# Perceiver block on one Trainium2 core: where the first contexts are loaded and turned, and in which order the queries are folded

## Chip, core and metric

The kernel runs on one core of a Trainium2 chip. The metric is the device time of one execution in microseconds (us). Three runs of the kernel before gave 2559.17, 2561.69 and 2563.82 us; the median is 2561.69 us.

## What is computed

A block of three residual steps on x (32 sequences of 64 tokens, 256 channels), with a context of 1601 tokens of 192 channels for each sequence, all in float32:

```python
x = x + xattn(layernorm(x), ctx_768)   # 16 heads of 64; q from x, k and v from the context
x = x + attn(layernorm(x))             # RWKV-like scan over time, three 256x256 projections in, one out
x = x + ffn(layernorm(x))              # 256 -> 1024 -> 256 with relu
```

Here only the first step matters. For each sequence and head it is softmax(q k^T / 8) v, with q = layernorm(x) w_q, and k, v from ctx_768 w_kv.

## The kernel before

**Folding.** The kernel never forms the keys. It multiplies each head's query by that head's key weights once, which gives a folded query of 192 channels (128 "lo" and 64 "hi" ones), and scores it against the raw context. This is `queries`, called once for each group of 8 sequences (`tg` 0 to 3), in two halves of 8 heads (`e` 0 and 1). Each half, called (tg,e) below, is on TensorE: 4 query projections into PSUM tag "ps" (L292, 2 buffers, copied by ScalarE to `room[1]`, L299), the lo folding (L313, PSUM tag "f" with 6 buffers, two for each head pair, copied by VectorE, L320, and ScalarE, L321, into one of two `q_lo` buffers), scores of the single last context token (`odd_scores`, L250, from group 1 on once in each half, and twice in (0,1)), and the hi folding (L341, copied at L348 to L352). The folded queries go to DRAM (`q_dram`) by SyncE: two stores of 1 MB for lo (L323), numbered lo0 to lo15 over the whole folding, and two of 0.5 MB for hi (L355). In the second half the next group's normalised x is turned (`turned_x`, L208, L211); `normed_x` of the group after that (L119, L110, L197) is queued on VectorE behind that copy.

**Attention.** 64 units `u` (32 sequences b, two halves of the heads j). `scores` runs 6 steps of matmuls (L658) of the turned context `cT` with the folded query `q`; ScalarE copies each step to `s_sb` (L665, two buffers, tag "s_sb"), VectorE keeps a running maximum (L667, L669). At the first step of a sequence `rest_scores` (L635) does the keys that don't fill a block. Then the maximum over partitions on GpSimd (L684), subtraction (L703) and exp (L704); one unit later `av_lo` (L468) and `av_hi` (L864) multiply by the context `c`, framed by `left` (L809, L819). `total` (L766 to L770) and `inverse` (L784 to L788) make the denominators, and `keep` (L794) sends them to DRAM from ScalarE's queue.

**Loads.** `blocks_load` (L170, 12 transfers, 1.2 MB in pieces of 128 bytes) brings the context as 32x32 blocks `cb`; `ctx_prep` turns them on VectorE (L372 three times, L373 once) into `cT` and ends with a small transfer from partitions 64-127 to 0-63 (L374). `ctx_load` (L143) brings `c`, 1.15 MB; `rows_load` (L152) four small transfers; `q_load` (L180) 1.5 MB of folded queries.

**What sets the order.** All these transfers are issued by SyncE, in one queue, in order. Each engine also executes a fixed list in order. A compiler's scheduler makes that list: it takes what it thinks is ready, and the kernel constrains it by `tc.issue_after(ins)`, which puts what the block traces on the same engine behind `ins` in that engine's list, without a wait for its end. The folding's queries may run ahead of the folding itself: nothing holds L292 of the next half back but its PSUM buffers and `room[1]`.

**Memory.** `room` is the two `s_sb` buffers before the attention needs them. The odd scores `od` use one of the two `cT` buffers; so only `cT` of sequence 0 is turned within the folding, and that of sequence 1 in unit 1. The four stores of each half of the last group's odd scores (L264) are put off (`odd_late`) until unit 0's other loads have been issued.

Of the kernel before, what the change touches and what calls it, by code (L numbers as in the profile page):

```python
# [9 lines left out]
F32 = mybir.dt.float32  # L10
# [5 lines left out]
P = 128  # L16
# [4 lines left out]
def kernel(  # L21
# [38 lines left out]
    nc = tc.nc  # L60

    B, T, D = x.shape
# [63 lines left out]
    with ExitStack() as st_b:  # L126
        with ExitStack() as st_a:
# [20 lines left out]
            def rows_load(b):  # L148

                for r0 in (0, C2):  # L150
                    for n, cs in ((0, slice(0, P)), (1, slice(P, C))):
                        nc.sync.dma_start(  # L152
                            rows[b % 2][r0 : r0 + KR, n, n * C2 : P], ctx_768[b, KC * P : NK - 1, cs]
                        )

            def blocks_load(b):

                c = cpool.tile([P, NS, NBL, BL], F32, tag="cb", name=f"cb_{b}")
                for k in range(2):
# [78 lines left out]
            def odd_scores(tg, e, kodT, qTs, od, sps):  # L242

                po = [
                    sps.tile([P, TG], F32, tag="f", name=f"odd_ps_{tg}_{e}_{o}", bufs=6)
                    for o in range(2)
                ]
                for k in range(4):
                    for o in range(2):
                        nc.tensor.matmul(  # L250
                            po[o][k * B : (k + 1) * B, :],
                            lhsT=kodT[o * HD : (o + 1) * HD, 4 * e + k, :],
                            rhs=qTs[k // 2][o * HD : (o + 1) * HD, k % 2, :],
                            start=True,
                            stop=True,
                        )
                nc.vector.tensor_copy(od[:, 0, :], po[0])
                nc.scalar.copy(od[:, 1, :], po[1])
# [9 lines left out]
            def queries(tg, xnT, copied, sp, sps, wq_sb, wkT, room, codn, kodT, wk_lo, wk_hi, od):  # L268
# [7 lines left out]
                for e in range(NP // 4):  # L276
# [5 lines left out]
                    for g in (2 * e, 2 * e + 1):  # L282
                        slot = (tg * NP // 2 + g) % 5
                        qT = room[1][:, slot * 2 * TG : (slot + 1) * 2 * TG].rearrange(
                            "p (k t) -> p k t", k=2
                        )
                        qTs.append(qT)
                        for k in range(2):
                            hp = 2 * g + k
                            pq = sps.tile([P, TG], F32, tag="ps", name=f"q_ps_{tg}_{hp}")  # L290
                            for c in range(2):
                                projected = nc.tensor.matmul(  # L292
                                    pq,
                                    lhsT=wq_sb[:, c, hp * P : (hp + 1) * P],
                                    rhs=xnT[:, c, :],
                                    start=(c == 0),
                                    stop=(c == 1),
                                )
                            nc.scalar.activation(qT[:, k, :], pq, AF.Copy, scale=HD**-0.5)  # L299
                    if e == 0 and tg == 0:  # L300
                        with tc.issue_after(projected.ins):
# [24 lines left out]
                        )  # L326
                    all_q.append(qTs)
                    for n in (0, 1) if e == 1 and tg == 0 else (e,) if tg else ():
                        odd_scores(tg, n, kodT, all_q[n], od[n], sps)
                        if more:  # L330
                            odd_store(tg, n, od[n])
                        else:
                            odd_late.append(lambda n=n: odd_store(tg, n, od[n]))
                    for k in range(2):
                        ph = [
                            sps.tile([P, QB, T], F32, tag="f", name=f"qh_ps_{tg}_{e}_{k}_{o}", bufs=6)
                            for o in range(2)
                        ]
                        for n in range(2):
                            for o in range(2):  # L340
                                nc.tensor.matmul(  # L341
                                    ph[o][n * C2 : (n + 1) * C2, :, :],
                                    lhsT=wkT[o * HD : (o + 1) * HD, 4 * e + 2 * n + k, P:C],
                                    rhs=qTs[n][o * HD : (o + 1) * HD, k, :],
                                    start=True,
                                    stop=True,
                                )
                        nc.vector.tensor_copy(hi[:, :, 2 * k, :], ph[0])  # L348
                        if e == 1 and not more:
                            nc.scalar.copy(hi[:, :, 2 * k + 1, :], ph[1])  # L350
                        else:
                            nc.vector.tensor_copy(hi[:, :, 2 * k + 1, :], ph[1])  # L352
                    for n in range(2):
                        ns = slice((8 * e + 4 * n) * T, (8 * e + 4 * n + 4) * T)
                        store = nc.sync.dma_start(  # L355
                            q_dram[tg][:, P:C, ns].rearrange("b p n -> p b n"),
                            hi[n * C2 : (n + 1) * C2].rearrange("p b h t -> p b (h t)"),
                        )
                    if e == 0 and tg == 0:
                        pk = sps.tile([P, NP, BL], F32, tag="f", name="kod_ps", bufs=6)  # L360
                        turned_keys(kodT, wk_lo, wk_hi, pk)
                return following, store

            def ctx_prep(b):
# [12 lines left out]
            with tc.tile_pool(name="setup", bufs=1) as sp, tc.tile_pool(  # L377
# [11 lines left out]
                ]  # L389
                wk_hi, codn = wk_hi[0:C2], codn[0:B]  # L390
                kodT = kodT.rearrange("p (h b) -> p h b", b=B)
                od = kp.tile([P, NS * KT], F32, tag="cT", name="od")
                od = [
                    od[:, k * 2 * TG : (k + 1) * 2 * TG].rearrange("p (o t) -> p o t", o=2)
                    for k in range(2)
                ]
                wq_sb = wq_sb.rearrange("p (c n) -> p c n", c=2)
                wkT = wkT.rearrange("p (h c) -> p h c", c=C)
                wqr = w_q.rearrange("(c p) n -> p c n", p=P)
# [10 lines left out]
                for n in range(4, NT, 4):  # L410
                    nc.sync.dma_start(x_sb[:, n : n + 4, :], xr[:, n : n + 4, :])
                b_tiles = {0: blocks_load(0)}
                odd_late = []
                for g in range(NP // 2):
                    ps = sps.tile([P, 2, C], F32, tag="ps", name=f"wkT_ps_{g}")
                    for k in range(2):
# [8 lines left out]
                for tg in range(B // QB):  # L425
                    turned, store = queries(tg, *turned, sp, sps, wq_sb, wkT, room, codn, kodT, wk_lo, wk_hi, od)
                    if tg == 1:
                        q_tiles = {0: q_load(0)}
                        cT = ctx_prep(0)

            nats = {}
            aw = st_a.enter_context(tc.tile_pool(name="late", bufs=1))
# [528 lines left out]
                        x_sb[:, i, :], x_sb[:, i, :], bias_rows[:, 0, :], ALU.add  # L961
                    )

            c_tiles = {}
            rests = [None, None]
            last = None
            before = None
# [2 lines left out]
            for u in range(2 * B):  # L970
# [2 lines left out]
                phase, i = (u - 5) % 4, (u - 5) // 4  # L973
                if before is not None:
                    before.out()
                if j == 0:
                    rows_load(b)
                out, mixer, older = outs[max(i, 0)], mixers[max(i, 0)], mixers[max(i - 1, 0)]
                fill = {}
# [18 lines left out]
                if u == 1:  # L998

                    hooks = {3: parts[0:2], 4: parts[2:3], 5: parts[3:]}  # L1000
                elif last is not None:
                    hooks = {
                        3: [last.inverse] + ([out.share] if phase == 1 and i >= 0 else []),
                        5: [last.keep],
                    }
                    last.total()
                else:
                    hooks = {}
                s_sb, mx, top, done = scores(u, cT, q_tiles[b], hooks)
                if j == 0 and b + 1 < B:  # L1010
                    with tc.issue_after(store.ins):
                        b_tiles[b + 1] = blocks_load(b + 1)
                        q_tiles[b + 1] = q_load(b + 1)
                mb = max_all(u, mx)
                if u == 1:
                    with tc.issue_after(top.ins):
                        cT_next = ctx_prep(1)
                if last is not None:
                    last.av_lo(fill, done)
                parts = exps(u, s_sb, rests[j], mb)  # L1020
# [4 lines left out]
                if u == 1:  # L1025
                    last.total()
                    last.inverse()
                    last.keep()
                if j == 0 and 0 < b < B - 1:
                    cT_next = ctx_prep(b + 1)  # L1030
                elif j == 1:
                    cT = cT_next
                if phase == 0 and i > 0:
# [4 lines left out]
                    out.vproj()  # L1038
                if phase == 1 and i >= 0:
                    mixer.norm()  # L1040
                if j == 0:
                    c_tiles[b] = ctx_load(b)
                if phase == 3 and i >= -1:
                    odd_load(i + 1)
# [150 lines left out]
```

## Time and profile before

| | us |
|---|---|
| median of three runs | 2561.69 |
| the profiled execution: its time | 2561.88 |
| its span (first to last instruction) | 2560.1 |
| TensorE busy in the span | 2536.7 (99%) |
| VectorE busy | 1925.9 (75%) |
| ScalarE busy | 985.5 (38%) |
| GpSimd busy | 410.7 (16%) |
| folding: first query projection to first score matmul | 13.07 to 136.10 |
| first score matmul of unit 2 | 192.59 |
| first score matmul of unit 4 | 266.59 |

"PE" is TensorE's matmul row, "PEld" its weight loads, "DVE" VectorE, "ACT" ScalarE, "POOL" GpSimd, "SP" SyncE (a "q" behind an engine is its instruction queue). In a timeline row the columns are start in us, duration in us, engine, line, operation, output<-input, shapes, count; in brackets stand the engine's idle time before it and what ended it. A float32 matmul leaves several records, so a count is of records. In a row of stretches the columns are the stretch, its length, each engine's busy time with its number of instructions, then the clock granted to TensorE (1.00 is full), the busy share of the DMA engines (it can exceed 1 where packets overlap), and GB/s.

### The profile page before, as it was taken

What the parts mean: (1) busy time and instruction counts of PE and PEld (TensorE: products, weight loads), DVE (VectorE), ACT (ScalarE), POOL (GpSimd) and SP (SyncE); (2) the same over time, 40 slices, a digit from 0 to 9 for tenths busy, and PEclk for the clock granted to TensorE, in tenths of its full rate; (3) what the DMA queues carried; (4) which work ended last, traced back from release to release, by engine and by line L of the source; (5) the groups of instructions that cost most, each with busy time, mean ns of one, the idle gap of its engine ahead of it and who ended that gap; (6) DMA issues with size and microseconds to landing.
All of it is one profiled execution on the core that took longest, in us unless ns stands there. A gap on an engine that the chain in (4) does not pass through costs nothing.

```text
span 2560.1 us, 38115 instructions
## 1 busy us (share of the span) xinstructions
PE 2536.7 (99%) x15618; PEld 1216.5 (48%) x15618; DVE 1925.9 (75%) x2364; ACT 985.5 (38%) x1103; POOL 410.7 (16%) x372
## 2 busy tenths in 40 slices
PE   9989999999999999999999999999999999999999
PEld 3344444444444454444444444444444444444466
DVE  5477778878787878878787878778787878787731
ACT  3343434434333444343443334344343334343221
POOL 1002111111111111111111111111111111211100
PEclk9999999999999999999999999999999999999999
DMA  8796333233332323233332323323332322210100
GB/s 209 218 207 110 61 62 65 48 66 65 62 63 59 58 42 66 47 66 66 65 66 53 69 43 55 67 48 65 66 65 55 67 59 52 54 47 2 52 13 21
DMA packets 435967, 174.23 MB, mean 68 GB/s; under 512 B 334960, under 2 KB 421520, under 8 KB 435792
## 3 DMA queue, kind: packets, MB, share of 16 engines
q1 hardware_dynamic: 435408, 171.53, 33.1%
q8 instruction: 122, 2.00, 0.3%
q14 instruction: 53, 0.43, 0.1%
q10 hardware_dynamic: 384, 0.26, 0.0%
HBM read 141.07 MB, written 29.10 MB: 66 GB/s over the span
## 4 chain that ended last, share of the span: by engine, by line
PE 91%; DVE 3%; issue 2%; DMA 1%; SPq 1%; POOL 1%; ACT 1%; DVEq 0%; ACTq 0%; POOLq 0%
PE s_ps L658 36%; PE o_lo L468 24%; PE o_hi L864 12%; PE y_ps L468 3%; PE q_ps L292 2%; PE h_ps L1106 2%; PE fy L1120 2%; PE rest_ps L635 2%; PE o_hi L819 1%; PE v_ps L917 1%; PE ql_ps L313 1%; PE o_lo L809 1%; DVE s_sb L703 1%; PE v_ps L931 1%; DVE m L669 1%
## 5 line engine op out<-in xcount | busy, mean ns | idle before, releaser
L658 PE MATMUL s_ps<-q,cT 64*128 64x512 f32 x4608 | 1009.3, 591 | 1.2 <-ACT q_hi L350 0.8
L658 PEld LDWEIGHTS s_ps<-q,cT 64*128 64x128 f32 x4608 | 444.1, 187 | 516.1 <-issue 498.3
L468 PE MATMUL o_lo<-s_sb,c 128*64 128x512 f32 x3024 | 678.5, 596 | 5.6 <-DMA c<-in_ctx_dram 5.6
L665 ACT COPY s_sb<-s_ps 128x1024 f32<-128x1024 f32 x384 | 388.3, 1011 | 743.9 <-PE s_ps L658 735.8
L703 DVE TENSOR_TENSOR s_sb<-s_sb,mb 128x2048 f32<-128x2048 f32 x192 | 431.7, 2285 | 0.0
L704 ACT ACTIVATE s_sb<-s_sb 128x2048 f32<-128x2048 f32 x192 | 367.1, 1912 | 123.4 <-DVE s_sb L703 123.4
L468 PEld LDWEIGHTS o_lo<-s_sb,c 128*64 128x64 f32 x3024 | 209.2, 137 | 386.9 <-issue 382.7
L669 DVE TENSOR_TENSOR m<-m,s_sb 128x1024 f32<-128x1024 f32 x256 | 312.4, 1220 | 45.2 <-ACT s_sb L665 23.3
L864 PE MATMUL o_hi<-s_sb,c 128*64 128x256 f32 x3024 | 337.0, 379 | 0.0
L769 DVE TENSOR_TENSOR t<-t,s_sb 128x1024 f32<-128x1024 f32 x256 | 312.1, 1219 | 8.6 <-DVE t L769 0.5
L864 PEld LDWEIGHTS o_hi<-s_sb,c 128*64 128x64 f32 x3024 | 217.3, 137 | 135.9 <-issue 35.9
L772 POOL PARTITION_ALL_REDUCE den<-t x64 | 207.1, 3236 | 401.1 <-issue 375.5
L784 DVE STREAM_TRANSPOSE turned<-den 128x512 f32<-128x512 f32 x64 | 45.5, 712 | 270.1 <-POOL den L772 270.1
L693 ACT ACTIVATE rest<-rest 128x512 f32<-128x512 f32 x64 | 40.4, 631 | 400.8 <-DVE rest L692 354.2
L684 POOL PARTITION_ALL_REDUCE mb<-m x64 | 114.2, 1785 | 423.8 <-DVE m L677 415.8
L692 DVE TENSOR_TENSOR rest<-rest,mb 128x512 f32<-128x512 f32 x64 | 44.3, 693 | 108.0 <-POOL mb L684 107.9
L623 POOL MEMSET rest<- 64x256 f32 x128 | 39.2, 307 | 416.8 <-PE o_lo L809 320.9
L372 DVE STREAM_TRANSPOSE cT<-cb 128x768 f32<-128x768 f32 x96 | 89.5, 958 | 0.0
L667 DVE TENSOR_TENSOR m<-s_sb 128x1024 f32<-128x1024 f32 x64 | 76.1, 1189 | 10.6 <-ACT s_sb L665 10.6
L819 PE MATMUL o_hi<-rest,rows 64*128 64x256 f32 x252 | 81.1, 402 | 0.0
L809 PE MATMUL o_lo<-rest,rows 64*128 64x256 f32 x252 | 81.1, 402 | 0.0
L111 POOL TENSOR_TENSOR rstd_ln<-rstd_ln,root 128x1 f32<-128x1 f32 (+1 forms) x24 | 33.1, 1379 | 295.1 <-DVE rstd_ln L110 277.2
(164 smaller groups left out, 1834.1 us busy)
## 6 DMA issues: line engine op xcount, KB each, us to landing
q<-q_dram SPq DMA_DIRECT2D x64, 768.0 KB
c<-in_ctx_dram SPq DMA_DIRECT2D x32, 1152.0 KB
cb<-in_ctx_dram SPq DMA_DIRECT2D x192, 104.0 KB
cb<-in_ctx_dram SPq DMA_DIRECT2D x192, 96.0 KB
q_dram<-q_lo SPq DMA_DIRECT2D x16, 1024.0 KB
q_dram<-q_hi SPq DMA_DIRECT2D x16, 512.0 KB
rows<-in_ctx_dram SPq DMA_DIRECT2D x64, 32.0 KB
rest<-o_dram SPq DMA_DIRECT2D x128, 1.0 KB
```

The source lines that it names most:

```text
L468: last = nc.tensor.matmul(out[rs], lhsT=lhsT[:, rs], rhs=rhs, start=start, stop=stop, skip_group_check=True,)
L658: done = nc.tensor.matmul(ps[:, k, :], lhsT=cT[rs, s, i * P : (i + 1) * P], rhs=q[rs, s, js : js + HALF], start=(s == 0), stop=(s == NS - 1),)
L665: copied = nc.scalar.copy(s_sb[:, 2 * i : 2 * i + 2, :], ps)
L669: nc.vector.tensor_tensor(m2, m2, s_sb[:, 2 * i : 2 * i + 2, :], ALU.max)
L684: nc.gpsimd.partition_all_reduce(mb, mx, P, bass_isa.ReduceOp.max)
L703: nc.vector.tensor_tensor(s, s, m, ALU.subtract)
L704: nc.scalar.activation(s, s, AF.Exp)
L769: nc.vector.tensor_tensor(t2, t2, p[:, 2 * i : 2 * i + 2, :], ALU.add)
L772: nc.gpsimd.partition_all_reduce(self.den, t2[:, 0, :], P, bass_isa.ReduceOp.add)
L809: nc.tensor.matmul(self.po[:, k * HH : (k + 1) * HH], lhsT=self.rows[lo, 0, :], rhs=self.rest[lo, k * HH : (k + 1) * HH], start=(k == 0), ...
L819: nc.tensor.matmul(self.ph, lhsT=self.rows.rearrange("p n c -> p (n c)")[hi, c0 : c0 + P], rhs=self.rest[hi, (1 - k) * HH : (2 - k) * HH], ...
L864: nc.tensor.matmul(self.ph[o * C2 : (o + 1) * C2, :], lhsT=self.ctx[:, self.at[c], P:C], rhs=self.s_sb[:, c, o * HH : (o + 1) * HH], start ...
```

## The change

- The queries of a half are put behind the last hi folding matmul of the half before it on TensorE (`folds`).
- The blocks of sequence 1 are loaded behind the first half's hi stores, into a buffer of tag "q" instead of "cb", and no more in unit 0.
- The odd scores leave the `cT` buffer: the first half of them goes to the buffer of tag "m2" (for the last group to a free slot of `room[1]`), the second to the end of `room[1]`. Thus both `cT` buffers are free, and `ctx_prep(0)` and `ctx_prep(1)` are both done in the folding, behind the last hi copies of VectorE (`filed`) of group 1 and group 2.
- `rows_load(0)` and `ctx_load(0)` are issued behind the stores of the third group (tg 2) and no more in unit 0.
- Of the last group's odd scores the first half is stored at once; only the second is still put off.
- `keep` of unit 0 moves from the end of unit 1 to the third score copy of unit 2; `ctx_prep(2)` is put behind the last maximum of unit 2.

```diff
-            def blocks_load(b):
-                c = cpool.tile([P, NS, NBL, BL], F32, tag="cb", name=f"cb_{b}")
+            def blocks_load(b, room=None):
+                if room is None:
+                    c = cpool.tile([P, NS, NBL, BL], F32, tag="cb", name=f"cb_{b}")
+                else:
+                    c = room.rearrange("p s n -> p (s n)")[:, 0 : NS * NBL * BL].rearrange(
+                        "p (s m r) -> p s m r", s=NS, r=BL
+                    )
...
-                            for c in range(2):
-                                projected = nc.tensor.matmul(
+                            with tc.issue_after(folds[-1].ins) if folds else ExitStack():
+                                for c in range(2):
+                                    projected = nc.tensor.matmul(
...
+                        if not more and n == 0:
+                            at = (tg * NP // 2 - 1) % 5 * 2 * TG
+                            od[0] = room[1][:, at : at + 2 * TG].rearrange("p (o t) -> p o t", o=2)
                         odd_scores(tg, n, kodT, all_q[n], od[n], sps)
-                        if more:
+                        if more or n == 0:
                             odd_store(tg, n, od[n])
...
-                                nc.tensor.matmul(
+                                fold = nc.tensor.matmul(
                                     ph[o][n * C2 : (n + 1) * C2, :, :],
...
-                        nc.vector.tensor_copy(hi[:, :, 2 * k, :], ph[0])
+                        filed.append(nc.vector.tensor_copy(hi[:, :, 2 * k, :], ph[0]))
...
+                    folds.append(fold)
...
+                        cb = kp.tile([P, NS, H * T], F32, tag="q", name="cb_1")
+                        with tc.issue_after(store.ins):
+                            b_tiles[1] = blocks_load(1, cb)
...
-                od = kp.tile([P, NS * KT], F32, tag="cT", name="od")
-                od = [
-                    od[:, k * 2 * TG : (k + 1) * 2 * TG].rearrange("p (o t) -> p o t", o=2)
-                    for k in range(2)
-                ]
+                m2 = ap.tile([P, 2, HALF], F32, tag="m2", name="od")
+                od = [m2, room[1][:, 10 * TG : 12 * TG].rearrange("p (o t) -> p o t", o=2)]
...
                     if tg == 1:
                         q_tiles = {0: q_load(0)}
-                        cT = ctx_prep(0)
+                    if tg in (1, 2):
+                        with tc.issue_after(filed[-1].ins):
+                            cTs[tg - 1] = ctx_prep(tg - 1)
+                    if tg == 2:
+                        with tc.issue_after(store.ins):
+                            rows_load(0)
+                            c_tiles = {0: ctx_load(0)}
...
-            c_tiles = {}
+            cT, cT_next = cTs[0], cTs[1]
...
-                if j == 0:
+                if j == 0 and b:
                     rows_load(b)
...
+                    if u == 2:
+                        hooks[2] = [before.keep]
...
-                        b_tiles[b + 1] = blocks_load(b + 1)
+                        if b:
+                            b_tiles[b + 1] = blocks_load(b + 1)
                         q_tiles[b + 1] = q_load(b + 1)
...
-                if u == 1:
-                    with tc.issue_after(top.ins):
-                        cT_next = ctx_prep(1)
...
                 if u == 1:
                     last.total()
                     last.inverse()
-                    last.keep()
                 if j == 0 and 0 < b < B - 1:
-                    cT_next = ctx_prep(b + 1)
+                    with tc.issue_after(top.ins) if b == 1 else ExitStack():
+                        cT_next = ctx_prep(b + 1)
...
-                if j == 0:
+                if j == 0 and b:
                     c_tiles[b] = ctx_load(b)
```

More of the change, by code (lines that the diff above doesn't have):

```diff
@@ L290, in queries @@
                             pq = sps.tile([P, TG], F32, tag="ps", name=f"q_ps_{tg}_{hp}")
-                            for c in range(2):
[L292 to L298, printed above, removed]
+                            with tc.issue_after(folds[-1].ins) if folds else ExitStack():
+                                for c in range(2):
+                                    projected = nc.tensor.matmul(
+                                        pq,
+                                        lhsT=wq_sb[:, c, hp * P : (hp + 1) * P],
+                                        rhs=xnT[:, c, :],
+                                        start=(c == 0),
+                                        stop=(c == 1),
+                                    )
                             nc.scalar.activation(qT[:, k, :], pq, AF.Copy, scale=HD**-0.5)
@@ L412 @@
                 b_tiles = {0: blocks_load(0)}
-                odd_late = []
+                odd_late, cTs, folds, filed = [], {}, [], []
                 for g in range(NP // 2):
```

## The prediction

> **What bounds the kernel now.** I read the busy times first: PE is busy 99% of the span, so a gain must come from PE's idle time or slowed matmuls. Next, PE's waits, longest first (us in total, times, longest):
>
> ```profile
> PE o_lo L468 <- DMA c<-in_ctx_dram: 5.6, 1, 5.6
> ...
> PE rest_ps L635 <- DMA cT<-cT: 2.1, 1, 2.1
> ...
> PE ql_ps L313 <- DVE q_lo L320: 1.0, 1, 1.0
> ```
>
> The first two are what the change aims at. PE's timeline places them in units 1 and 2:
>
> ```profile
> 168.98 0.38 PE L819 MATMUL o_hi<-rest,rows 64*128 64x256 f32 x1
> 174.97 11.97 PE L468 MATMUL o_lo<-s_sb,c 128*64 128x512 f32 x48 [5.62 <-DMA c<-in_ctx_dram]
> 186.76 5.36 PE L864 MATMUL o_hi<-s_sb,c 128*64 128x256 f32 x48
> ...
> 192.59 2.74 PE L658 MATMUL s_ps<-q,cT 64*128 64x512 f32 x12
> 197.44 1.95 PE L635 MATMUL rest_ps<-q,cT 64*64 64x256 f32 x24 [2.11 <-DMA cT<-cT]
> ```
>
> The queue of SyncE (SP) explains both: `c` is issued only at 161.02, behind rows, blocks and q_1; the transfer ending `ctx_prep(1)` at 195.19, behind all late loads. Stretches of 1 us show what follows a gap (column after POOL: granted clock):
>
> ```profile
> 175.00:176.00 1.00, 1.00 (x4) 0.42 (x6) 1.00 (x2) 0.00 (x0) 0.00 (x0) 0.50 0.18 27
> ...
> 199.00:200.00 1.00, 1.00 (x6) 0.50 (x4) 0.99 (x3) 0.55 (x2) 0.00 (x0) 0.50 0.08 17
> 200.00:201.00 1.00, 1.00 (x4) 0.34 (x2) 0.97 (x2) 0.91 (x3) 0.00 (x0) 0.50 0.01 1
> ```
>
> Each gap is followed by some 3 us at half clock. Last the folding, PE and then VectorE (DVE):
>
> ```profile
> 36.62 2.84 PE L313 MATMUL ql_ps<-room,room 64*128 64x512 f32 x10
> 39.39 4.56 PE L292 MATMUL q_ps<-xnT,room 128*128 128x512 f32 x10
> ...
> 69.90 1.13 PE L292 MATMUL q_ps<-xnT,room 128*128 128x512 f32 x2
> 70.96 1.12 PE L313 MATMUL ql_ps<-room,room 64*128 64x512 f32 x2
> 73.13 1.12 PE L313 MATMUL ql_ps<-room,room 64*128 64x512 f32 x2 [1.05 <-DVE q_lo L320]
> ```
>
> ```profile
> 39.11 0.17 DVE L110 TENSOR_SCALAR rstd_ln<-mv_ln 128x4 f32<-128x4 f32 x1
> 40.48 0.41 DVE L197 TENSOR_SCALAR xn_in_k<-x_sb,mv_ln,rstd_ln 128x256 f32<-128x256 f32 x1 [1.19 <-POOL rstd_ln L111]
> ...
> 41.77 1.88 DVE L320 COPY q_lo<-ql_ps 128x512 f32<-128x512 f32 x3
> ```
>
> From 37.34 to 41.77 DVE does the next group's `normed_x`, and the finished lo foldings wait for it. Three pairs fill the 6 PSUM buffers by 39.39; PE goes on only because it may take the next half's queries, which the change forbids.
>
> **Gain in units 1 and 2.** From the last `left` matmul to the first o_lo takes 0.31 us elsewhere (283.92 to 284.23), so o_lo could start at 169.29: 5.68 us. Its 48 records take 11.79 (174.97 to 186.76) against 10.45 in an undisturbed unit (chain, from 317.62): 1.34. The 12 score records need 2.68 (266.59 to 269.27), so rest_ps could start at 195.27, not 197.44: 2.17. From there to the end of unit 2's scores 16.08 (to 213.52) against 14.43 (269.27 to 283.70): 1.65. Sum 10.84. All of it is on the path: after 215 PE shows no idle time until the last units, and the first context's exps end at 172.6, ahead of what o_lo needs (its last third, about 176). Against it: `total(0)` must be through with `s_sb` (190.3 now) and unit 2 starts 7 us sooner; the turning removed from DVE (2.69 + 0.38, from 177.48) gives back 3.07, leaving about 187.2 against a first copy at 188.2. ScalarE would reach that copy beside exps(1): I take 0.5 lost (0 to 2). `keep(0)`, which stood ahead of this copy (197.70 against 197.95), is moved to the third, when the denominator is ready; left in place it would cost some 2 us. Net 10.3.
>
> **The folding, TensorE.** In strict order a first half costs 6.97 for queries (27.48 to 34.45), 3.63 lo (51.47 to 55.10), 1.02 odd, 1.88 hi: 13.50. A second half has turning amid lo, 4.94 (34.45 to 39.39) plus 1.06 for the last pair: 15.87, or 16.72 in group 0 with two odd scores. From 13.07: (0,0) ends at 27.48, then 16.72 + 4 x 13.50 + 2 x 15.87 gives 129.94, with the PSUM handover of 0.83 130.8. Now it is 136.1, since lo pairs are torn apart (two records alone cost 1.06, as four do) and PE waits 1.05 and 1.22.
>
> But the cover for `normed_x` is gone. In (0,1) PE stops at 39.39 until DVE's first lo copy frees a buffer: that starts at 41.77, and in (1,1) PE resumed 0.74 after such a start: 42.51, so 3.12. In (1,1) 69.90 to 73.13: 3.23. `normed_x` stays ahead of these copies, as what decides it at that point is not touched. In (2,1) no `normed_x` follows. Sum 6.35 (0 if the order turns out otherwise).
>
> Do such stalls halve the clock? [...] Rule: 0; row: 2 x 1.5 (mean of 1.34 and 1.65). I take the row, +3.0. The folding then ends at 140.1, 4.0 later than now.
>
> **The folding, transfers.** Added are the blocks (1.2 MB), `c` (1.15 MB) and rows. What SP's queue carries (last columns: DMA share, GB/s):
>
> ```profile
> 112.00:116.00 4.00, 4.00 (x38) 1.04 (x38) 2.40 (x4) 1.25 (x3) 0.00 (x0) 1.00 1.04 341
> 120.00:124.00 4.00, 3.13 (x8) 1.10 (x6) 0.53 (x1) 1.70 (x4) 0.00 (x0) 1.00 0.99 208
> 156.00:160.00 4.00, 4.00 (x22) 1.82 (x20) 2.02 (x3) 2.02 (x2) 1.80 (x1) 1.00 1.37 124
> 84.00:88.00 4.00, 4.00 (x16) 1.19 (x14) 2.08 (x3) 1.76 (x3) 0.00 (x0) 1.00 0.98 216
> ```
>
> Lo stores run at 341, hi stores at 208, blocks at about 130, q at 216. So a half is 2.1 MB lo 6.3 us, 1.05 MB hi 5.0, odd 0.5: 11.8 of 13.5 to 16.7; q_0 7.3, blocks 9.5 (SP is held 8.5, as from 150.85, to 14.0, as from 8.45), `c` and rows 5.7. Blocks are issued behind the hi stores at 30.4, when the DMA engines would run dry (0.00 in 36 to 40); all to hi of (1,0) is through by 69, while lo6 is ready only about 78. From there a queue builds: lo6, lo7, odd, hi 90; q_0 97; lo8, lo9 103; odd, hi 109; lo10, lo11 115; odd, hi 121; rows, c 126; lo12, lo13 132.6. A lo copy needs its buffer's store two numbers earlier landed (1.5 more): lo15's at about 135.3 needs lo13 at 134.1. It fits by 1.2 us: cost 0, up to 4 if transfers are 5% slower over these 55 us and the clock drops. VectorE's two `ctx_prep` (3.07 each) lie where it idles for the next half's queries (5.67 before 84.50); uncovered, they would cost 3 each.
>
> **Behind the folding.** The last odd half's four stores read `room[1]`, which unit 1's first copy overwrites (now 156.10, then about 160.1; PE bears 1.56 more). SP issues them behind hi, rest and q_1: about 158.5 landed. Cost 0; eight took 14.14 us to issue behind a full queue, so up to 4.
>
> **Sum.** -10.84 + 0.5 + 4.0 = -6.3: span 2560.1 to 2553.8; around it lie 1.78 us, so 2555.6, and the profiled run stands 0.19 above the median: 2555.4.
>
> **Rivals.**
> - No stall: DVE's list has the lo copies ahead of `normed_x`, or the scheduler hides it. -10.84 - 5.3 + 0.5 gives 2546. Against: nothing before that point differs.
> - Late stores of `od` or `keep` hold unit 1 or 2: 4 us more, 2559.5. For: the 14.14 us. Against: `c`, rows and blocks no longer stand ahead.
> - Slower: the DMA queue paces the folding. From lo6 on all is back to back, and each late store stops PE without queries to fall back on. If all 15.2 us of added transfers come through, plus 3 of clock, less the 1.2 of slack and 2 that overlap the stalls: +15, 2570. It decides once the 55 us stretch by 2%, and reaches "slower" at some 20%. For: lo copies wait 1.17 and 1.32 us for stores even now. Against: the transfer-free stretches (36 to 44, 104 to 112), which the even order uses.
> - The change doesn't remove the waits: `c` would have to be 30 us late; under 2%.
>
> **Numbers.** About 0.2% (5.1 us) is what a measurement of this kernel can tell from no change: faster is below 2556.6, slower above 2566.8. As computed 0.50 (2551 to 2559.5; two thirds of it faster); no stall 0.18, faster; late stores 0.17 (2557 to 2563); DMA-paced 0.15 (2566 to 2580), nearly all slower. Faster 0.55, same 0.30, slower 0.15. Range 2546 to 2567.
>
> **What would show it.** Right: PE's waits without `c` and `cT`; q_ps in blocks of 16; two PE gaps of about 3 us <-DVE q_lo near 40 and 73, each followed by 0.50 clock; first scores near 140, unit 2 near 189.5. Wrong: lo copies waiting for q_dram stores over 2 us, a gap at unit 1's start, or a folding over by 132.

## The result, and the profile after

| | before | after |
|---|---|---|
| median | 2561.19 (21 runs, 2559.17 to 2566.04) | 2565.4 (21 runs, 2560.29 to 2566.93) |
| ratio to before, 95% interval | | 1.0014 [1.0008, 1.0019] |
| the profiled execution: time, span | 2561.88, 2560.1 | 2564.72, 2562.9 |
| first score matmul of unit 0 | 136.10 | 143.11 |
| of unit 2 | 192.59 | 196.99 |
| of unit 4 | 266.59 | 268.30 |

2555.4 us was predicted, 0.25% faster. The changed kernel is 0.14% slower: small, but clear of the spread of the runs. In the changed kernel L319 is the lo folding, L326 and L327 are its copies, L202 the end of `normed_x`, L676 the scores, L683 their copies, L722 the exps, L714 the small stores of `left` and L812 those of `keep`.

TensorE's waits, read first again, over the whole span (us in total, times, longest):

```profile
PE ql_ps L319 <- DVE q_lo L326: 5.8, 2, 2.9
...
PE o_lo L486 <- ACT s_sb L722: 2.6, 1, 2.6
...
PE s_ps L676 <- ACT s_sb L683: 1.3, 3, 0.8
PE rw_ps_Wr L500 <- ACT Wk_T L505: 1.1, 1, 1.1
```

The waits for `c` and `cT`, 5.6 and 2.1 us before, are gone, so the change does what it says. Four waits stand in their place. The first was foreseen; the other three were not in the sum. (The waits left out stand at the start and the end of the kernel, before the change too.) TensorE's timeline shows where they are:

```profile
37.78 2.97 PE L319 MATMUL ql_ps<-room,room 64*128 64x512 f32 x12
43.67 2.07 PE L319 MATMUL ql_ps<-room,room 64*128 64x512 f32 x2 [2.92 <-DVE q_lo L326]
45.67 3.66 PE L255 MATMUL odd_ps<-room,room 64*32 64x512 f32 x32
...
80.23 1.37 PE L319 MATMUL ql_ps<-room,room 64*128 64x512 f32 x2 [2.92 <-DVE q_lo L326]
...
143.11 2.85 PE L676 MATMUL s_ps<-q,cT 64*128 64x512 f32 x12 [0.84 <-ACT q_hi L360]
...
182.56 8.78 PE L486 MATMUL o_lo<-s_sb,c 128*64 128x512 f32 x32 [2.61 <-ACT s_sb L722]
196.99 2.74 PE L676 MATMUL s_ps<-q,cT 64*128 64x512 f32 x12
220.81 0.66 PE L500 MATMUL rw_ps_Wr<-ident,nat_Wr 128*128 128x128 f32 x4 [1.06 <-ACT Wk_T L505]
273.25 13.14 PE L676 MATMUL s_ps<-q,cT 64*128 64x512 f32 x60 [0.76 <-ACT s_sb L683]
```

Two gaps of 2.92 us lie in the second halves of groups 0 and 1, one of 2.61 us in unit 1, and two small ones in units 2 and 4 (1.06 and 0.76). The stretches show the clock behind the first two (column after POOL):

```profile
40.00:44.00 4.00, 1.08 (x5) 0.33 (x2) 2.77 (x10) 0.97 (x2) 1.01 (x1) 0.93 1.32 138
44.00:48.00 4.00, 4.00 (x26) 0.82 (x33) 1.69 (x4) 0.83 (x2) 0.00 (x0) 0.50 1.15 265
48.00:52.00 4.00, 4.00 (x33) 0.94 (x18) 2.22 (x4) 0.93 (x2) 0.00 (x0) 0.72 0.96 308
80.00:84.00 4.00, 3.77 (x22) 0.82 (x26) 2.39 (x5) 0.97 (x2) 0.00 (x0) 0.62 0.57 184
```

From 44 to 48 TensorE is busy throughout, at a clock of 0.50. VectorE's timeline has the cause of the gap, as forecast:

```profile
41.63 0.41 DVE L202 TENSOR_SCALAR xn_in_k<-x_sb,mv_ln,rstd_ln 128x256 f32<-128x256 f32 x1 [1.19 <-POOL rstd_ln L111]
...
42.93 2.48 DVE L326 COPY q_lo<-ql_ps 128x512 f32<-128x512 f32 x4
```

The lo copies stand behind `normed_x` in VectorE's list; TensorE resumes 0.74 us after the first of them starts.

The gap in unit 1 was not forecast. ScalarE's timeline:

```profile
163.63 1.01 ACT L683 COPY s_sb<-s_ps 128x1024 f32<-128x1024 f32 x1 [2.09 <-DMA o_dram<-room]
...
172.28 1.90 ACT L722 ACTIVATE s_sb<-s_sb 128x2048 f32<-128x2048 f32 x1
178.93 0.71 ACTq L714 DMA_DIRECT2D pd_dram<-rest  x2
179.69 1.01 ACT L683 COPY s_sb<-s_ps 128x1024 f32<-128x1024 f32 x1 [5.51 <-DMA pd_dram<-rest]
180.59 1.91 ACT L722 ACTIVATE s_sb<-s_sb 128x2048 f32<-128x2048 f32 x1
```

Between two exps of unit 0 stands the issue of two 1 KB stores, of `left`, and ScalarE stood before them from 174.18, the end of the first exp, to 178.9. The chain of waits says what let them go:

```profile
176.27 2.59 DMA b_sb<-in_L_ffn_b_dram
178.86 0.02 issue
178.88 0.02 ACTq L714
178.89 0.04 issue
178.93 0.72 DMA pd_dram<-rest
179.65 0.04 issue
179.69 1.02 ACT s_sb L683
```

The store was issued 0.02 us after an unrelated load of SyncE, that of a bias vector issued at 176.27, had landed, and the chain has this landing as what let it go. Why a store of ScalarE's queue stands behind that load is not shown by any run. In the kernel before the same store was issued at 165.39, within the first exp, without a wait:

```profile
165.26 1.90 ACT L704 ACTIVATE s_sb<-s_sb 128x2048 f32<-128x2048 f32 x1
165.39 0.71 ACTq L696 DMA_DIRECT2D pd_dram<-rest  x2
```

There `c`, rows and blocks were still loaded in unit 0. In the changed kernel they no longer are, and the load that the chain names is the last of the loads of weights and biases. Whether the one brought about the other is not shown.

### The profile page after: what moved, and what is told of

Same layout as the page of the kernel before. It is cut to its first block, busy times and chain, and to the rows that moved or that the text cites. A ratio compares the mean times of both kernels' runs of the same rounds, so it can differ in the third digit from the quotient of the medians.

```text
span 2562.9 us, 38106 instructions
## 1 busy us (share of the span) xinstructions
PE 2538.8 (99%) x15618; PEld 1215.4 (47%) x15618; DVE 1927.7 (75%) x2364; ACT 986.2 (38%) x1103; POOL 412.3 (16%) x372
## 4 chain that ended last, share of the span: by engine, by line
PE 90%; DVE 3%; issue 2%; DMA 1%; POOL 1%; SPq 1%; ACT 1%; ACTq 0%; DVEq 0%; POOLq 0%
PE s_ps L676 36%; PE o_lo L486 24%; PE o_hi L882 11%; PE y_ps L486 2%; PE h_ps L1124 2%; PE fy L1138 2%; PE q_ps L298 2%; PE rest_ps L653 2%; PE o_hi L837 1%; PE ql_ps L319 1%; PE v_ps L935 1%; DVE s_sb L721 1%; PE o_lo L827 1%; PE v_ps L949 1%; POOL den L790 1%
## 5 line engine op out<-in xcount | busy, mean ns | idle before, releaser
L676 PE MATMUL s_ps<-q,cT 64*128 64x512 f32 x4608 | 1008.0, 590 | 2.2 <-ACT s_sb L683 1.3
L676 PEld LDWEIGHTS s_ps<-q,cT 64*128 64x128 f32 x4608 | 443.5, 187 | 516.3 <-issue 497.7
L683 ACT COPY s_sb<-s_ps 128x1024 f32<-128x1024 f32 x384 | 388.3, 1011 | 731.4 <-PE s_ps L676 723.8
L722 ACT ACTIVATE s_sb<-s_sb 128x2048 f32<-128x2048 f32 x192 | 367.1, 1912 | 123.9 <-DVE s_sb L721 123.8
```

The source lines that it names most:

```text
L676: done = nc.tensor.matmul(ps[:, k, :], lhsT=cT[rs, s, i * P : (i + 1) * P], rhs=q[rs, s, js : js + HALF], start=(s == 0), stop=(s == NS - 1),)
L683: copied = nc.scalar.copy(s_sb[:, 2 * i : 2 * i + 2, :], ps)
L722: nc.scalar.activation(s, s, AF.Exp)
```

## The experiments

"First", "unit 2" and "unit 4" are the starts of the first score matmul of units 0, 2 and 4. The ratio is to the kernel before, with its 95% interval. The starts are those of one profiled execution each. From the first score of unit 5 to the end the profiled executions take 2256.3 to 2258.8 us (2258.5 before, 2258.8 after); what sets this difference isn't known, so a difference of 2 us in time alone says little about the stages named here.

| kernel | first | unit 2 | unit 4 | median | ratio |
|---|---|---|---|---|---|
| before | 136.10 | 192.59 | 266.59 | 2561.19 | 1 |
| after | 143.11 | 196.99 | 268.30 | 2565.4 | 1.0014 [1.0008, 1.0019] |
| e1_ahead | 147.23 | 202.66 | 272.84 | 2567.5 | 1.0024 [1.0017, 1.0032] |
| e2_norm | 132.76 | 189.60 | 260.91 | 2553.87 | 0.9972 [0.9962, 0.9983] |
| e3_store | 142.26 | 192.81 | 263.76 | 2559.87 | 0.9993 [0.9985, 1.0001] |
| e4_order_only | 139.43 | 190.04 | 270.89 | 2563.53 | 1.0007 [0.9999, 1.0016] |
| e5_both | 132.86 | 182.92 | 254.37 | 2548.78 | 0.9950 [0.9937, 0.9964] |
| e6_den2 | 142.63 | 196.24 | 266.42 | 2565.25 | 1.0014 [1.0007, 1.0020] |
| e7_all | 132.25 | 181.61 | 252.94 | 2551.86 | 0.9963 [0.9951, 0.9976] |
| e8_before_norm | 142.13 | 198.99 | 271.10 | 2565.39 | 1.0015 [1.0009, 1.0022] |
| f1_once | 132.39 | 181.75 | 253.89 | 2548.9 | 0.9950 [0.9938, 0.9963] |
| f2_ahead | 153.85 | 203.35 | 275.35 | 2570.37 | 1.0035 [1.0021, 1.0048] |
| f3_late_c | 131.54 | 187.22 | 258.40 | 2552.59 | 0.9966 [0.9953, 0.9978] |
| f4_late_cb | 131.68 | 190.38 | 261.70 | 2557.37 | 0.9983 [0.9974, 0.9991] |
| g1_keep | 143.31 | 197.93 | 275.36 | 2570.97 | 1.0037 [1.0023, 1.0051] |
| g2_keep_both | 131.43 | 182.80 | 260.35 | 2554.51 | 0.9972 [0.9960, 0.9983] |

**The folding: is the order the loss, or what stands in VectorE's list?** First the hold on the queries is taken out of the changed kernel:

```diff
-                            with tc.issue_after(folds[-1].ins) if folds else ExitStack():
+                            with ExitStack():
```

> The changed kernel without the hold on the query projections (they may run ahead of the folding again); everything else stays. Theory A (the strict order removed the cover of normed_x, and the stalls halve the clock: 2 x 2.9 us of waiting plus 4.9 us of slow matmuls): the two waits for q_lo copies shrink to about 1 us, no half clock near 45 and 81, the first score matmul comes at 136 to 138 instead of 143.1, and the time falls by 3 to 6 us, to about 2560. Rival B (the added transfers pace the folding): the first score stays at 141 or later, lo copies wait for q_dram stores, time within 1.5 us of 2565.

A miss: the first scores came 4.1 us later than with the hold, and the lo copies wait for stores, as rival B had it. The stretches of this kernel (last columns: DMA share, GB/s) show it:

```profile
60.00:64.00 4.00, 3.69 (x15) 1.79 (x13) 1.31 (x3) 1.19 (x2) 0.00 (x0) 1.00 0.00 0
64.00:68.00 4.00, 4.00 (x10) 1.82 (x10) 2.78 (x13) 1.53 (x3) 1.01 (x1) 1.00 0.00 0
```

While queries run ahead nothing is folded, so nothing can be stored: 8 us without a byte. The stores pile up later, where a copy of ScalarE waits 9.4 us for one, and TensorE 4.8 for that copy. With the added loads the even order is worth more than it costs. Next, the hold stays, and `normed_x` is put behind the last hi copy on VectorE:

```diff
-                        with tc.issue_after(copied.ins):
+                        with tc.issue_after(filed[-1].ins if filed else copied.ins):
```

> The changed kernel, strict order kept, but normed_x queued on VectorE behind the last hi copy of the half before instead of behind the turned x. Theory A: both q_lo waits and both half-clock stretches vanish, 5.8 + 4.9 us, first score near 132.5; the stores of q and of the odd scores end less much earlier, so some of it is given back at unit 1; time about 2558 (2555 to 2561). Rival B (transfers pace the folding): TensorE waits for stores instead, first score at 138 or later, time 2562 or more.

Right: both gaps are gone, the first scores come at 132.76, 10.4 us earlier. VectorE's timeline in this kernel:

```profile
38.44 2.09 DVE L326 COPY q_lo<-ql_ps 128x512 f32<-128x512 f32 x3
...
46.77 0.74 DVE L119 BATCH_NORM_STATS2 st_ln<-x_sb 128x6 f32<-128x256 f32 x2
```

The copies come at once; `normed_x` follows at 46.77, beside the next half's queries. In unit 1 the wait for the store is still there (3.63 us). Then the hold alone, in the kernel before:

```diff
-                            for c in range(2):
+                            with tc.issue_after(folds[-1].ins) if folds else ExitStack():
+                                for c in range(2):
...
-                                nc.tensor.matmul(
+                                fold = nc.tensor.matmul(
...
+                    folds.append(fold)
```

> The kernel before with only the hold on the query projections added: no moved loads. Theory A: the folding is as slow as in the changed kernel, first score at 141 to 143, the waits for c and cT stay or shrink a little since the folding's stores end no later, time 2565 to 2569. Rival B (the added transfers, not the order, lengthen the folding): first score at 136 or earlier, time 2561 or less.

Partly: the first scores came at 139.43, after a single gap of 2.92 us (43.51). In group 1 no such gap appeared: there three of the lo copies stand between the steps of `normed_x` in VectorE's list (73.90, 76.26 and 77.76), and TensorE waited only 0.99 us, at 81.04. `c` made TensorE wait 1.2 us, `cT` 3.7, and a copy of scores 3.6 more. And `normed_x` alone is moved in the kernel before, where queries run ahead:

```diff
-                        with tc.issue_after(copied.ins):
+                        with tc.issue_after(filed[-1].ins if filed else copied.ins):
...
-                        nc.vector.tensor_copy(hi[:, :, 2 * k, :], ph[0])
+                        filed.append(nc.vector.tensor_copy(hi[:, :, 2 * k, :], ph[0]))
```

> The kernel before with only normed_x moved behind the last hi copy; queries may run ahead there. Theory A (normed_x costs only where no queries can fill in): at most the 1.05 us wait near 72 and one torn pair go, time 2559 to 2561.5. Rival: normed_x ahead of the lo copies was a cost in the kernel before too, time 2556 or less.

A miss: 2565.39 us, 0.15% slower than before, with the first scores 6.0 us later. TensorE's timeline shows one cause:

```profile
58.96 1.84 PE L313 MATMUL ql_ps<-room,room 64*128 64x512 f32 x2 [2.96 <-DVE q_lo L320]
```

With queries ahead, the next half's lo folding is what collides with the moved `normed_x`; behind the wait the next 16 odd and 16 hi records take 1.96 and 3.63 us (1.09 and 1.95 in the kernel before, from 55.10). Neither edit alone gained anything. The same holds from the other side, in the kernel with both repairs (below) but no hold:

```diff
-                            with tc.issue_after(folds[-1].ins) if folds else ExitStack():
+                            with ExitStack():
```

> Both repairs, but the query projections may run ahead of the folding again. Theory A (with the block loads and the first context in the folding, queries that run ahead leave the transfers idle and the stores of their low halves then pile up): the first score comes at 138 to 147 us, the copies of the low halves wait 3 us or more for their stores, 2555 to 2563. Rival B (the order held nothing up; all that mattered was the normalization's place): first score at 132 to 134, 2547 to 2551.

The direction of A, but far more: 21.6 us above `e5_both`, 21.0 of them before the first score. Its TensorE timeline names two of the places:

```profile
97.21 0.66 PE L213 MATMUL xnT_ps<-ident,xn_in_k 128*128 128x128 f32 x2 [5.55 <-DVE xn_in_k L202]
...
146.53 2.20 PE L319 MATMUL ql_ps<-room,room 64*128 64x512 f32 x4 [7.57 <-ACT q_lo L327]
```

The moved `normed_x` is now late for the turning of x, and a copy of ScalarE waits 10.9 us for a store.

**ScalarE behind the small store.** In the changed kernel the two stores of `left` of unit 0 are put behind the last exp; only their place in ScalarE's list changes:

```diff
+                    if u:
+                        kept()
+
+                def kept():
...
-                return [left] + parts
+                return [left] + parts + ([] if u else [kept])
```

> The changed kernel, with unit 0's two pd_dram stores on ScalarE's queue moved behind its last exp. Theory A (these stores wait 5.5 us for the completion of an earlier transfer, a load on SyncE's queue that ends at 178.9, and hold the exps behind them): the 2.6 us wait of o_lo and the half clock after it (1.65) vanish, unit 2 starts near 192.7, time lower by about 4.3, near 2561. Rival C (the exps are late by themselves, or the wait moves to the next thing in the queue): no change, 2565.

Right in cause: the time is 5.5 us less than after. Of the 5.2 us between the two profiled executions 3.3 lie in units 0 and 1 (50.55 us instead of 53.88), where the edit acts; 0.9 lie ahead of the first score, where it changes nothing; that part of the gain is luck. The weighted sums of unit 0 in TensorE's timeline are whole again:

```profile
176.65 10.52 PE L486 MATMUL o_lo<-s_sb,c 128*64 128x512 f32 x48
```

Both repairs together (`e2_norm` and `e3_store`):

> The changed kernel with both repairs: normed_x behind the last hi copy, unit 0's pd_dram stores behind its last exp. Theory A (two separate costs): they add up, first score near 132.8 as with the first alone, no wait of o_lo for the exps, time about 5 below the first repair alone, near 2549 (2547 to 2551). What stays is the wait of unit 1's first copy for the odd scores' stores (1.7 us of TensorE). Rival D (the transfers' end sets units 1 and 2 anyway): the gain of the second is absorbed, time 2552 to 2554.

Right: 2548.78 us, 0.9950 [0.9937, 0.9964] of before. The repairs add up (11.5 and 5.5 each alone, 16.6 together).

**What is lost from unit 2 on.** `keep` of unit 0, now issued at the third copy of unit 2, sends the denominators off at 206.72; the store lands at 214.37, and GpSimd's next denominators, which use the same tile, wait for it:

```profile
214.56 3.55 POOL L790 PARTITION_ALL_REDUCE den<-t  x1 [11.54 <-DMA pd_dram<-rden]
```

Next in line are the inverse, unit 1's `keep`, and ScalarE's copies of turned weights behind it: the 1.06 us at 220.81. First the tile got a second buffer:

```diff
-                    self.den = aw.tile([P, HALF], F32, tag="den", name=f"den_{u}")
+                    self.den = aw.tile([P, HALF], F32, tag="den", name=f"den_{u}", bufs=2)
...
-                    self.rden = aw.tile([P, HALF // BL, BL], F32, tag="den", name=f"rden_{u}")
+                    self.rden = aw.tile([P, HALF // BL, BL], F32, tag="den", name=f"rden_{u}", bufs=2)
```

> The changed kernel with two buffers for the denominators (tag den) instead of one, so that unit 1's sum over partitions need not wait until unit 0's denominators have been stored by the moved keep. Theory E (the moved keep, which lands only at 214.4, delays unit 1's denominators and through ScalarE's queue the turning of the weights): the waits of rw_ps_Wr (1.1) and of s_ps in unit 4 (0.8) vanish, time lower by 1.5 to 2, near 2563.5. Rival: these two waits have another cause, no change (2565 to 2566).

A miss. The wait of 1.06 us goes, but TensorE waits longer in unit 4 (2.40 us, after 0.76):

```profile
273.01 13.14 PE L676 MATMUL s_ps<-q,cT 64*128 64x512 f32 x60 [2.40 <-ACT s_sb L683]
```

There ScalarE makes the last exps of unit 3 until 272.06, and the first copy of unit 4 stands behind them. Why they are later than in the changed kernel isn't settled. All repairs at once, with the last odd scores stored at once too:

> The changed kernel with four repairs: normed_x behind the last hi copy, unit 0's pd_dram stores behind its last exp, two den buffers, and the last odd scores stored at once instead of late. If each of the named waits is what cost the time, TensorE shows none of them, first score near 133, unit 2 about 50 us later, time 2544 to 2548. If an unnamed cause (run-to-run place of memory, more traffic) holds part of it, 2549 or more.

A miss again: unit 4 starts at 252.94, 1.4 us ahead of `e5_both`, but there TensorE waits 3.42 us:

```profile
260.56 13.15 PE L676 MATMUL s_ps<-q,cT 64*128 64x512 f32 x60 [3.42 <-ACT s_sb L683]
```

Unit 5 starts 1.2 us behind that of `e5_both`; where the rest of the 3.1 us comes from isn't settled. Since these two runs did not show what the moved `keep` costs, it was put back to the end of unit 1, in the changed kernel and in `e5_both`:

```diff
-                    if u == 2:
-                        hooks[2] = [before.keep]
...
                     last.inverse()
+                    last.keep()
```

> The changed kernel, with the keep of unit 0 at the end of unit 1 again. Theory A (the prediction's step: left there, it holds ScalarE's first copy of scores of unit 2 until the denominators are ready): a wait of 1 to 3 us on the copies of scores at unit 2, time 2566 to 2568. Theory B (moved to the third copy of unit 2, its store lands late, the next denominators wait for that, and unit 2 and unit 4 lose 2 us by it): the waits of the turned weights and of the scores in unit 4 go, time 2562.5 to 2564.5. Rival E (as with two den tiles, what is saved there comes back as a wait in unit 4): 2565 to 2566.

> Both repairs (normalization behind the last hi copy, unit 0's small stores behind its last exp), with the keep of unit 0 at the end of unit 1 again. Unit 2 starts at about 183 us there. Theory A: the keep waits for the denominators and ScalarE's first copy of unit 2 behind it, 1 to 3 us more, 2550 to 2552. Theory B: the wait of 0.9 us of the turned weights and that of 0.8 us in unit 4 go, 2546.5 to 2548. Rival E: no difference within 0.7 us, 2548 to 2549.5.

Theory A, but at about twice the most that it allowed: 5.6 and 5.7 us slower. ScalarE's timeline of `g2_keep_both`:

```profile
191.54 0.20 ACTq L816 DMA_DIRECT2D pd_dram<-rden  x1
191.79 1.01 ACT L683 COPY s_sb<-s_ps 128x1024 f32<-128x1024 f32 x1 [6.82 <-DVE rden L810]
```

The first copy of unit 2 stands behind the `keep`, which waits for the denominators; TensorE waits 5.85 us for it, and its next 60 records take 14.59 instead of 13.15. B's mechanism shows in the same runs: the 1.1 us wait for the turned weights and the 0.8 us in unit 4 are gone (from unit 4 to unit 5 it takes 34.97 and 34.98 us, as before the change, and 35.80 after it). So the moved `keep` costs some 1.9 us where it stands (1.1 and 0.8), and would cost 7.3 where it stood (5.85 of wait and 1.44 of slow matmuls). The difference, 5.4, is about what the two runs lost.

**The odd scores, and what the early loads are worth.** In `e5_both`, ScalarE's first copy of unit 1 still waits 3.5 us for stores of `od`. Now they are sent one by one:

```diff
-                        if more or n == 0:
+                        if True:
```

> Both repairs, and the last odd scores of unit 0 stored one by one as they come instead of all behind the last one. Theory A (the remaining wait at the start of unit 1 is ScalarE's first copy of scores, which waited 3.5 us behind stores of the odd part): that wait goes or shrinks below 1.5 us, TensorE's 0.8 us waits on the copies of scores at unit 1 go, nothing later changes: unit 2's first score 182.0 to 182.6, time 2547 to 2548.5. Rival E (a small shift of ScalarE's order in unit 1 only moves the wait, as with two den tiles): a wait of 2 to 3.4 us on the copies of scores in unit 4, time 2549 to 2552.

Between the two theories: ScalarE's wait goes, and unit 2 starts 1.2 us earlier, of which 0.5 was there at the first score. The time is that of `e5_both`: a wait of 0.9 us comes in unit 2 (0.2 in `e5_both`), and what remains at unit 4 (0.5) is too little for these runs to tell. Then one early load at a time is put back into unit 0, in `e5_both`. First the context:

```diff
-                    if tg == 2:
-                        with tc.issue_after(store.ins):
-                            rows_load(0)
-                            c_tiles = {0: ctx_load(0)}
...
-                if j == 0 and b:
+                if j == 0:
                     rows_load(b)
...
-                if j == 0 and b:
+                if j == 0:
                     c_tiles[b] = ctx_load(b)
```

> Both repairs, with the first context's rows loaded in unit 0 again, behind the first scores, as in the kernel before. Theory A (the early load is what took the wait of 2.4 us for the context from unit 0's second half): the wait of the weighted sums for the context comes back at 1 to 4 us at the end of unit 0, first score 0 to 1 us earlier, time 2549 to 2552. Rival B (the folding stage is bound by its transfers, so that the 1 MB less there is worth more than the wait): first score 2 to 3 us earlier, time 2545 to 2548.

It is 3.8 us slower, just beyond A, but no wait for `c` came back (5.6 us in the kernel before, not the 2.4 of the expectation). ScalarE and SyncE in this kernel:

```profile
157.50 1.93 ACT L679 COPY s_sb<-s_ps 128x1024 f32<-128x1024 f32 x2 [7.51 <-DMA wv_lo<-in_L_xattn_w_kv_dram]
```

```profile
143.64 0.60 SPq L143 DMA_DIRECT2D c<-in_ctx_dram  x1
144.29 4.90 SPq L269 DMA_DIRECT2D o_dram<-room  x4
149.30 0.36 SPq L452 DMA_DIRECT2D wv_lo<-in_L_xattn_w_kv_dram  x1
```

`c` now stands ahead of the four stores of `od`, and the copy that overwrites `room[1]` has to wait for them. (The profile names the load issued right behind the stores, `wv_lo`; that the copy waits for the stores follows from the program, which has `od` in `room[1]`.) TensorE waits 4.49 us at unit 1's scores. Last, blocks and turning of sequence 1 go back:

```diff
-                        cb = kp.tile([P, NS, H * T], F32, tag="q", name="cb_1")
-                        with tc.issue_after(store.ins):
-                            b_tiles[1] = blocks_load(1, cb)
...
-                    if tg in (1, 2):
+                    if tg == 1:
...
-                        if b:
-                            b_tiles[b + 1] = blocks_load(b + 1)
+                        b_tiles[b + 1] = blocks_load(b + 1)
...
+                if u == 1:
+                    with tc.issue_after(top.ins):
+                        cT_next = ctx_prep(1)
```

> Both repairs, with the second batch's blocks loaded in unit 0 and turned in unit 1 again; the first context stays early. Theory A (the wait for the turned second context in unit 2 comes from its late blocks, and the early load is worth it): the wait of the scores for the turned context comes back at 2 to 5 us at unit 2, with a slow stretch behind it, first score within 1 us of that with both repairs, time 2552 to 2556. Rival B (with unit 0's transfers relieved of the first context, the blocks land early enough even from there): no wait in unit 2, time 2546 to 2549, and the folding stage 0 to 2 us shorter.

8.6 us slower than `e5_both`, and without the wait of theory A: unit 2 shows none for `cT`. The twelve block loads hold the stores of `od` even longer (their issue starts at 150.12, after 144.29 in `f3_late_c`; ScalarE waits 10.2 us, TensorE 7.2 at unit 1's scores). So what both runs show as the cost of a late load is that it stands ahead of the stores of `od`, which are now out of `room[1]`. By the author's estimate `c` was in time by itself: the copy that waits for the stores behind it in the queue starts at 157.50, and `c` is first read at 171.06, without a wait. Whether `cT` would be is not shown, since TensorE had been held 7.2 us before. Two things were not run: these two kernels with the odd scores sent one by one as in `f1_once`, which sends the stores ahead of unit 0's loads (132.79 there), and the hold with the moved `normed_x` without any early load. What the early loads together are worth is therefore not measured.

## Why the prediction was wrong

The sum was -6.3 us of span; it is +2.8. Of the 9.1 us between them 3.0 lie ahead of the first score, 4.4 in units 0 and 1, 1.7 behind.

- *Gain in units 1 and 2*: right in what goes (5.68 and 2.17, with their slow stretches), wrong in that nothing comes instead. Unit 0 to unit 2 takes 53.88 us (196.99 - 143.11) where 56.49 - 7.02 = 49.47 was forecast. The step that failed is "the first context's exps end at 172.6, ahead of what o_lo needs". That was read from the trace of before, and the place of a store among these exps was not looked at; now the second exp starts at 180.59, held behind it, and TensorE stops at its second third. 2.61 us of wait and 1.7 of slow matmuls (8.6 us from 182.56 to the next matmul, against 6.97 by the 10.45 of an undisturbed unit; the clock was 0.50 from 184 to 186) are 4.3 of the 4.4. `e3_store`, which moves only the store, takes both away; 3.3 of the 4.4 come back there, since ScalarE then waits 3.96 us for the stores of `od`, and TensorE 0.93. That the store's place costs is shown; that it waited for the load of the bias vector rests on the 0.02 us and on the chain alone. The rival "late stores of `od` or `keep`" named the right kind of thing and the wrong store: in the changed kernel those of `od` held ScalarE 2.09 us and TensorE not at all (the 132 records of unit 0 and 1 take 28.59 us, 28.60 before).
- *The folding, TensorE*: mechanism right, size off. The two gaps came (2.92 each; 3.12 and 3.23 forecast). The term that was too small is the clock, "2 x 1.5": behind the first gap the matmuls took 3.1 us more, behind the second 1.6. For these two gaps the choice of the row was right: no run shows where the 0 beside it ("Rule: 0") comes from, and behind the gaps the clock was at 0.50 (44 to 50 and 81 to 84). Yet the row did not hold everywhere either: after the 2.40 us of `e6_den2` and the 3.42 us of `e7_all` nothing was lost (60 records in 13.14 and 13.15 us; 13.14 without a gap in the kernel before, from 270.72). The rest is in the first group, whose second queries start at 28.64 instead of 27.48: the first 16 query records start 0.31 us later and take 8.48 us against 7.62 (7.55 to 8.86 in the kernels shown here). No wait is shown and the clock column says 1.00, but until about 16.1 single records take up to 1.22 us, as at a clock of 0.50 elsewhere (1.06 and 1.22 behind the first gap, from 43.67), and 0.59 to 0.61 from there on; in the kernel before they do so only until 14.1. So TensorE started slow for longer; why stays open. The strict order itself is as computed: 28.64 to 143.11 is 114.5 us, and without the gaps (5.84) and the slow clock (4.7) it is 103.9, where 103.3 was forecast.
- *The folding, transfers*: right. Not one lo copy waits for a store (3.1 us on VectorE and 1.6 on ScalarE before), so the rival paced by transfers fell, though the time is close to the 2566 where it began; `e1_ahead` and `f2_ahead` show that this is owed to the even order.
- *Behind the folding*, the store of `od`: right within its bounds, landed at 163.5 instead of 158.5.
- *keep*: the prediction set the moved one at 0 and the unmoved at "some 2 us". `g1_keep` and `g2_keep_both` give 1.9 and 7.3. Moving it was worth more than forecast, but it was not free: 0.5 was allowed for behind unit 2 and 1.7 more came, and the 1.9 are most of these 2.2.
- The rival "no stall", 2546, is about what `e5_both` measures, 2548.78, with the 1.9 us of `keep` in it; but it needed two edits, as neither the list nor the scheduler hid `normed_x`.

## What to carry to other kernels

When work that ran ahead is held back, ask what else stood in the other engines' lists at that point: the queries had covered a normalisation, and only both edits together paid. And a small store in a compute engine's list was here a wait of 4.7 us, until a load of another queue had landed, where it had been issued without a wait before other loads were moved; so put such stores behind the work that someone waits for, which took 3.3 us out of units 0 and 1 in `e3_store`. A store moved off one engine's critical copy is still followed by whoever reuses its tile: here GpSimd stood idle for 11.54 us until `keep`'s store had landed.

## What was not expected of the hardware

- The length of a gap did not set its cost: after 2.92 us idle the slow clock cost 3.1 us in one place and 1.6 in another, after 2.61 us 1.7, and after 3.42 us (`e7_all`) and 2.40 us (`e6_den2`) nothing (60 records in 13.15 and 13.14 us).
- A 1 KB store of ScalarE's queue was held 4.7 us (174.18 to 178.88 in the changed kernel) and issued 0.02 us after an unrelated load of SyncE's queue had landed.
